# Delta-rule decoder on one core: a POOL inverse held behind the next pair's key norms, more buffers for queries and P, and join copies moved to ScalarE

## The chip, the cores and the metric

The kernel runs on one core of a Trainium2 chip. A core has a matrix engine (TensorE, in the profile PE, with its weight loads as PEld), a vector engine (VectorE, DVE), an activation engine (ScalarE, ACT), a general engine (GpSimd, POOL) and a queue engine that issues DMAs (SyncE, SP). Each engine works through its own list of instructions in the order that was fixed when the program was built; engines wait for each other by semaphores. The metric is device microseconds for one execution of the whole program, and lower is better.

## What is computed

One decoder layer on x of shape 4 x 512 x 512 in float32: a gated delta-rule attention with 16 heads of 128, then a cross attention to 256 context rows, then a causal attention, then a mixture of 8 experts. The change lies in the delta rule:

```python
def step(Sstate, inputs):
    q_t, k_t, v_t, g_t, beta_t = inputs
    retrieved = jnp.einsum('bhkv,bhk->bhv', Sstate, k_t)
    error = v_t - g_t[..., None] * retrieved
    update = k_t[..., :, None] * (beta_t[..., None] * error)[..., None, :]
    Snew = g_t[..., None, None] * Sstate + update
    o_t = jnp.einsum('bhkv,bhk->bhv', Snew, q_t)
    return (Snew, o_t)
...
o = o * jax.lax.rsqrt(jnp.mean(o * o, axis=-1, keepdims=True) + EPS) * norm_w
o = o * jax.nn.silu(x @ Wg.T)
return o @ Wo.T
```

q, k and v are projections of the normalised x, passed through a causal convolution of 4 taps and silu; q and k are scaled to length 1.

## The kernel before

The 512 steps of a sequence are done in 4 chunks of 128. Within a chunk the recurrence becomes a triangular system, and its inverse is a 128 x 128 matrix per chunk and head. Heads go in pairs: 4 sequences times 8 pairs make 32 pairs, numbered m. A pair passes through these stages:

- `stage1(m)`: the projections and convolutions of k and q. For k: projection, convolution (lines 503, 511, 514), silu, transposes (546), squares with a row sum (551), then the norms of k: `ss` on VectorE (557) and five small operations on GpSimd (558 to 562: `rk`, `ee`, `ee`, `ke`, `nr`). `ee` scales a decay matrix `em` on ScalarE (line 397, called from 572); from it and from k times k, VectorE makes `at` (579), the matrix to be inverted. It is stored to DRAM (580), and its 32 x 32 diagonal blocks are loaded as `iA` (633). Then come the q side, P (`pt`, 601), the gated q (`qg`, 590) and the norms of q (`rq`, 610 to 623).
- `stage2_inverse(m)`: 31 elimination steps on 32 partitions, each a multiplication (644) and an addition (645). Even pairs do them on VectorE, odd pairs on GpSimd. Then `iT` is stored (648), transposed by a copy (649) and stored (650), and whole squares are loaded back as `T` (653) and `X` (655).
- `stage2_values(m)`: the projections of v and of the gate (`gs`).
- `stage3(m)`: the joins put the 32 x 32 blocks together to a 128 x 128 inverse: four groups of small matmuls (704/705, 714/716, 727, 736) with copies between them (707/708, 718 to 720, 730, 738). The first group needs `T`, the second `X`. Then the row `rrow` with the norms of q is loaded (742), the gate is multiplied by it on GpSimd (745), and the four chunks follow (758 to 787), each a chain through TensorE, VectorE and ScalarE. Line 796 makes `og`.
- `output(m)`: the output projection of a pair (825), summed up in `xa`; after the last pair of a sequence, the scaling and the residual (843) and the store (845).

`prologue(b)` normalises the next sequence. Round m of the loop at line 920 writes out `stage3(m)` and, in turns with its steps, `output(m-1)`, `stage1(m+2)`, `stage2_values(m+1)` and `stage2_inverse(m+1)`: in each turn `stage1` and the inverse go two steps and the others one. The key norms of pair m+2 are written out in the sixth turn, ahead of that turn's inverse steps, which are numbers 10 and 11 of 31.

That is the order of the program. The framework's planner then fixes the list of each engine at build time: it goes by the order of the program, but puts a later instruction first where it expects an earlier one to be still waiting, by its own estimate of how long things take. So the elimination of pair m+1, which is ready early, runs about a round ahead of its place in the program. A tile name with `bufs=n` has n buffers, and a new tile waits until the last reader of the oldest is done.

Of the kernel before, what the change touches and what calls it, by code (L numbers as in the profile page):

```python
# [31 lines left out]
F32 = mybir.dt.float32  # L32
AF = mybir.ActivationFunctionType
ALU = mybir.AluOpType
# [4 lines left out]
P = 128  # L39
B, S, D = 4, 512, 512  # L40
NT = B * S // P
TB = S // P
# [56 lines left out]
def decoder(ctx: ExitStack, tc: tile.TileContext, a: dict, out: bass.AP):  # L99
# [39 lines left out]
    def chain(*gs):  # L139
        for g in gs:  # L140
            yield from g
# [27 lines left out]
    def idle(n):  # L169
        for _ in range(n):  # L170
            yield
# [154 lines left out]
    with ExitStack() as st:  # L326
# [64 lines left out]
        def chunks(t):  # L391
            return t.rearrange("p c j -> p (c j)")
# [8 lines left out]
        def prologue(b):  # L401

            x = []
            for c in range(TB):
                t = w2.tile([P, D], F32, name="x_in", bufs=4)
                nc.sync.dma_start(t, x_t[:, b * TB + c, :])
                x.append(t)
            yield
            yield
            for c, t in enumerate(x):  # L410
                run(layernorm(t.unsqueeze(1), t.unsqueeze(1), small))
                if c == 0:
                    xnT = s2.tile([P, KD, S], F32, name="xnT", bufs=2)
                    seqs[b] = [xnT]
                tp = p_b.tile([P, KD, P], F32, name="pb")
                for kd in range(KD):
                    nc.tensor.transpose(tp[:, kd, :], t[:, kd * P : (kd + 1) * P], ident)
                nc.scalar.copy(xnT[:, :, c * P : (c + 1) * P], tp)
                yield
            pab = p_b.tile([P, TB, 32], F32, name="pb")  # L420
# [101 lines left out]
        def stage1(m):  # L522
# [38 lines left out]
            nc.gpsimd.tensor_tensor(ke, ee, flat(gend), ALU.mult)  # L561
            nc.gpsimd.tensor_tensor(nr, ss, rk, ALU.mult)
            em = []
# [7 lines left out]
            for p in range(HG):  # L571
                scale(em[p], em[p], ee, p)
                pk = p_b.tile([P, TB, P], F32, name="pb")
                for c in range(TB):
                    k_ = kT[p][:, c * P : (c + 1) * P]
                    nc.tensor.matmul(pk[:, c, :], k_, k_, start=True, stop=True)
                at = live.tile([P, TB, P], F32, name="at", bufs=6)
                ats.append(at)
                nc.vector.scalar_tensor_tensor(at, pk, -1.0, em[p], ALU.mult, ALU.mult)  # L579
                nc.sync.dma_start(squares(at_d[m % SLOTS][p * TB : (p + 1) * TB]), at)  # L580
                yield
# [4 lines left out]
            for p in range(HG):  # L586
                q = s1.tile([P, S], F32, name="qh")
                yield from conv(b, hg, p, 0, wq, q)
                g = live.tile([P, S], F32, name="qg", bufs=4)
                nc.gpsimd.tensor_tensor(g, q, mb[p], ALU.mult)  # L590
                qg.append(g)
                t = w2.tile([P, S], F32, name="cv", bufs=5)
                nc.scalar.activation(t, q, AF.Square)
                sq.append(t)
                yield
                pq = p_b.tile([P, TB, P], F32, name="pb")
                for c in range(TB):
                    cs = slice(c * P, (c + 1) * P)
                    nc.tensor.matmul(pq[:, c, :], kT[p][:, cs], q[:, cs], start=True, stop=True)
                t = live.tile([P, TB, P], F32, name="pt", bufs=4)  # L600
                nc.vector.tensor_tensor(t, pq, em[p], ALU.mult)
                pt.append(t)
                yield
# [21 lines left out]

        inverses = {}

# [8 lines left out]
        def stage2_inverse(m):  # L636

            nb = HG * TB * 4
            A, T, W, ats = inverses.pop(m)
            eng = nc.vector if m % 2 == 0 else nc.gpsimd  # L640
            for i in range(31):
                n, w = 31 - i, i + 1
                u = W[:, : n * w].rearrange("p (a b) -> p a b", a=n)
                eng.tensor_tensor(u, A[:, i, i + 1 :].unsqueeze(2).to_broadcast([nb, n, w]), T[:, i, :w].unsqueeze(1).to_broadcast([nb, n, w]), ALU.mult)  # L644
                eng.tensor_tensor(T[:, i + 1 :, :w], T[:, i + 1 :, :w], u, ALU.add)  # L645
                yield
            dT, dX = inv_d[m % 2]
            nc.sync.dma_start(blocks(dT), T)
            eng.tensor_copy(A, T.rearrange("p t j -> p j t"))
# [3 lines left out]
            nc.sync.dma_start(t, squares(dT))  # L653
# [36 lines left out]
        def stage3(m):  # L690
# [15 lines left out]
            for p in range(HG):  # L706
                nc.vector.tensor_copy(Yd[p][32:64, :, 0:32], py[lo[p]])
                nc.scalar.copy(Yd[p][96:128, :, 32:64], py[hi[p]])
# [8 lines left out]
            for p in range(HG):  # L717
                nc.vector.tensor_copy(Ts[p][32:64, :, 0:32], px[lo[p], :, 64:96])
                nc.scalar.copy(Xs[p][0:32, :, 32:64], px[lo[p], :, 0:32])
                nc.vector.tensor_copy(Xs[p][64:96, :, 96:128], px[hi[p], :, 32:64])  # L720
            yield
# [21 lines left out]
            rb = [t[:, p, :] for p in range(HG)]  # L743
            for p in range(HG):
                nc.gpsimd.tensor_tensor(gs[p], gs[p], rb[p], ALU.mult)

            st_ = [None] * HG
            po = [p_o.tile([P, TB, P], F32, name=f"po{p}") for p in range(HG)]
            for c in range(TB):
# [34 lines left out]
                for p in range(HG):  # L784
                    nc.tensor.matmul(po[p][:, c, :], us[p], pt[p][:, c, :], start=True, stop=c == 0)
                    if c > 0:
                        nc.tensor.matmul(po[p][:, c, :], st_[p], qg[p][:, cs], start=False, stop=True)
                st_ = nst
                yield

# [19 lines left out]
        def output(m):  # L810
# [21 lines left out]
            if hg == NHG - 1:  # L832
# [8 lines left out]
                for c in range(TB):  # L841
                    xr = xs[c]
                    nc.vector.scalar_tensor_tensor(xr, xa[c], rs[:, c : c + 1], xr, ALU.mult, ALU.add)

                    (nc.gpsimd if m == NP - 1 else nc.sync).dma_start(x1d[b * TB + c], xr)
                    yield

        def prepare():

            ctx_ = [w2.tile([P, D], F32, name="og", bufs=2) for _ in range(2)]  # L850
            for kt in range(2):
                nc.sync.dma_start(ctx_[kt], a["ctx"][kt * P : (kt + 1) * P])
            wk = [w2.tile([P, D], F32, name="x_in", bufs=4) for _ in range(KD)]
            for kd in range(KD):
# [65 lines left out]
        for m in range(NP):  # L920
# [15 lines left out]
            if m:  # L936
                rest.append((output(m - 1), 1))
            if m + 2 < NP:
# [586 lines left out]
```

## Time and profile before

| what | value |
| --- | --- |
| time, median of 3 executions | 3873.22 us (3867.34 to 3873.66) |
| the profiled execution | 3875.28 us, its span 3873.5 us |
| busy: PE, DVE, ACT, POOL | 90%, 58%, 39%, 35% of the span |
| granted PE clock, mean over the span | 0.945 of full speed |
| part with the delta rule | from the start to about 2160 us |
| first join matmuls of pairs 2 and 30 | 272.0 us and 2078.5 us: 28 rounds in 1806.5 us |

The page gives busy times, the chain that ended last and groups of instructions. For a change to the order of work the views by time are of more use: the timeline of one engine, the list of who waited for whom in a stretch, and the busy time and granted clock by stretches. A wait of one engine costs time only where it ends in a wait of the engine that sets the pace.

### The profile page before, as it was taken

What the parts mean: (1) busy time and instruction counts of PE and PEld (TensorE: products, weight loads), DVE (VectorE), ACT (ScalarE), POOL (GpSimd) and SP (SyncE); (2) the same over time, 40 slices, a digit from 0 to 9 for tenths busy, and PEclk for the clock granted to TensorE, in tenths of its full rate; (3) what the DMA queues carried; (4) which work ended last, traced back from release to release, by engine and by line L of the source; (5) the groups of instructions that cost most, each with busy time, mean ns of one, the idle gap of its engine ahead of it and who ended that gap; (6) DMA issues with size and microseconds to landing.
All of it is one profiled execution on the core that took longest, in us unless ns stands there. A gap on an engine that the chain in (4) does not pass through costs nothing. (4 is left out here: it accounts for less than half of the span.)

```text
span 3873.5 us, 48929 instructions
## 1 busy us (share of the span) xinstructions
PE 3479.9 (90%) x16466; PEld 1984.5 (51%) x16466; DVE 2238.7 (58%) x5115; ACT 1523.7 (39%) x4190; POOL 1374.0 (35%) x1941
## 2 busy tenths in 40 slices
PE   5898989898989898989889879999999999898897
PEld 3455555555555555555545445555555555554443
DVE  5576657765766676657665546655665565554111
ACT  3334443334443434343433334444444444344121
POOL 1543554355335543554355222213212221211442
PEclk8899999998999999999999889999999999999898
DMA  5324332433234324333433245445544444456444
GB/s 163 109 71 126 104 103 78 130 104 114 78 106 129 104 77 120 105 102 100 120 88 111 72 154 161 139 147 158 163 132 140 145 139 141 137 174 206 82 82 92
DMA packets 391881, 465.56 MB, mean 120 GB/s; under 512 B 128451, under 2 KB 242115, under 8 KB 391440
## 3 DMA queue, kind: packets, MB, share of 16 engines
q1 hardware_dynamic: 380080, 438.03, 37.8%
q0 software_dynamic: 10112, 21.58, 3.1%
q8 instruction: 132, 2.16, 0.2%
q10 hardware_dynamic: 1440, 2.84, 0.2%
q14 instruction: 117, 0.96, 0.1%
HBM read 401.76 MB, written 64.81 MB: 120 GB/s over the span
## 5 line engine op out<-in xcount | busy, mean ns | idle before, releaser
L503 PE MATMUL pb<-xnT,w 128*128 128x512 f32 x2048 | 953.0, 604 | 0.0
L503 PEld LDWEIGHTS pb<-xnT,w 128*128 128x128 f32 x2048 | 381.0, 195 | 421.9 <-issue 417.8
L514 DVE SCALAR_TENSOR_TENSOR cv<-pb,pp,cv 128x511 f32<-128x511 f32 (+2 forms) x576 | 427.6, 742 | 153.0 <-ACT cv L511 144.0
L1067 PE MATMUL pb<-c_q,hT 128*128 128x512 f32 x768 | 360.7, 608 | 7.4 <-DMA c_q<-in_c_wq_dram 3.4
L644 POOL TENSOR_TENSOR iW<-iA,iT 32x31 f32<-32x31 f32 (+15 forms) x496 | 249.4, 503 | 212.3 <-DMA iA<-at_d 142.2
L825 PE MATMUL pb<-wot,og 128*128 128x512 f32 x512 | 265.9, 644 | 31.8 <-DVE og L796 26.5
L645 POOL TENSOR_TENSOR iT<-iT,iW 32x31 f32<-32x31 f32 (+15 forms) x496 | 275.2, 555 | 38.9
L511 ACT ACTIVATE cv<-pb,pp 128x512 f32<-128x512 f32 x192 | 148.2, 772 | 259.9 <-PE pb L503 259.4
L1173 PE MATMUL pw<-c_o,oT 128*128 128x512 f32 x512 | 241.8, 603 | 2.9 <-DVE oT L1165 2.9
L1067 PEld LDWEIGHTS pb<-c_q,hT 128*128 128x128 f32 x768 | 143.5, 195 | 165.4 <-issue 152.3
L1139 ACT ACTIVATE e<-pb,nm,rq 128x128 f32<-128x128 f32 (+3 forms) x256 | 157.0, 618 | 142.4 <-DVE nm L1137 108.8
L274 POOL TENSOR_SCALAR x_e<-x_e 128x1024 f32<-128x1024 f32 x64 | 68.7, 1074 | 329.4 <-ACT x_e L269 240.4
L644 DVE TENSOR_TENSOR iW<-iA,iT 32x31 f32<-32x31 f32 (+15 forms) x496 | 177.9, 359 | 12.4 <-DMA iA<-at_d 0.9
L645 DVE TENSOR_TENSOR iT<-iT,iW 32x31 f32<-32x31 f32 (+15 forms) x496 | 176.0, 355 | 11.9
L1163 PE MATMUL po<-eT,val 128*128 128x512 f32 x320 | 170.2, 625 | 6.9 <-ACT eT L1161 3.8
L558 POOL TENSOR_TENSOR rk<-ss,mhalf 128x8 f32<-128x8 f32 x32 | 53.1, 1658 | 317.9 <-DVE ss L557 317.8
L579 DVE SCALAR_TENSOR_TENSOR at<-pb,em 128x512 f32<-128x512 f32 x64 | 44.3, 692 | 208.5 <-ACT em L397 208.5
L1133 PE MATMUL pb<-kT,qT 128*128 128x256 f32 (+3 forms) x576 | 162.7, 409 | 0.8 <-ACT x_e L269 0.8
L269 ACT ACTIVATE x_e<-pb,nm 128x256 f32<-128x256 f32 x256 | 118.2, 477 | 101.9 <-DVE nm L266 101.9
L995 POOL TENSOR_TENSOR rope_s<-q,tab 128x128 f32<-128x128 f32 x64 | 35.4, 552 | 319.7 <-DVE q L1097 281.0
L825 PEld LDWEIGHTS pb<-wot,og 128*128 128x128 f32 x512 | 90.9, 197 | 110.3 <-issue 54.2
L397 ACT ACTIVATE em<-em,ee 128x128 f32<-128x128 f32 x256 | 78.6, 388 | 172.4 <-POOL ee L560 172.4
(324 smaller groups left out, 6742.1 us busy)
## 6 DMA issues: line engine op xcount, KB each, us to landing
c_o<-in_c_wo_dram SPq DMA_DIRECT2D x128, 512.0 KB, 4.1
c_q<-in_c_wq_dram SPq DMA_DIRECT2D x128, 512.0 KB, 4.7
w<-in_a_w_dram SPq DMA_DIRECT2D x124, 512.0 KB, 3.7
row<-g_d SPq DMA_DIRECT2D x64, 512.0 KB, 3.8
at_d<-at SPq DMA_DIRECT2D x64, 256.0 KB, 3.7
T<-t_d SPq DMA_DIRECT2D x32, 512.0 KB, 6.2
X<-x_d SPq DMA_DIRECT2D x32, 512.0 KB, 6.4
rrow<-r_d SPq DMA_DIRECT2D x32, 512.0 KB, 4.9
```

What stands on the lines that cost most here:

```text
L269: nc.scalar.activation(e[:, n, :], ps[r][:, g, :], AF.Exp, bias=nm[:, n : n + 1], accum_out=ssum[:, n : n + 1])
L503: nc.tensor.matmul(pj, wt[:, kd, p * P : (p + 1) * P], xnT[:, kd, :], start=kd == 0, stop=kd == KD - 1)
L511: nc.scalar.activation(ac, pj, AF.Identity, bias=cb[:, m, h : h + 1], scale=cw[:, m, h, 3:4])
L514: nc.vector.scalar_tensor_tensor(ac[:, j:], pj[:, : S - j], cw[:, m, h, 3 - j : 4 - j], ac[:, j:], ALU.mult, ALU.add)
L644: eng.tensor_tensor(u, A[:, i, i + 1 :].unsqueeze(2).to_broadcast([nb, n, w]), T[:, i, :w].unsqueeze(1).to_broadcast([nb, n, w]), ALU.mult)
L645: eng.tensor_tensor(T[:, i + 1 :, :w], T[:, i + 1 :, :w], u, ALU.add)
L825: nc.tensor.matmul(pw, og[p][:, c * P : (c + 1) * P], wot[:, p, :], start=p == 0, stop=p == HG - 1)
L1067: nc.tensor.matmul(pj, hT[:, kd, :], w[:, kd % 2, :], start=kd == 0, stop=kd == KD - 1)
L1133: nc.tensor.matmul(ps[:, m, k * P : (k + w) * P], qT[g][:, n + m, :], kT[:, g, j : j + w, :], start=True, stop=True)
L1139: nc.scalar.activation(e[n + m][:, :nk], ps[:, m, :nk], AF.Exp, bias=nm[:, n + m : n + m + 1], scale=rq, accum_out=es[:, n + m : n + m + 1])
L1163: nc.tensor.matmul(po, val[:, g, :], eT, start=k == 0, stop=k == c)
L1173: nc.tensor.matmul(pw, oT[:, h + m, :], w[:, m, :], start=g == 0 and h + m == 0, stop=g == 3 and h + m == 3)
```

## The change

Seven edits go together.

1. The last norm instruction of each pair (`nr`, 562) is remembered, and the elimination steps of odd pairs from 3 on are written out under `tc.issue_after(norms_[-1])`. That adds an edge of order alone: on GpSimd's list these steps come behind the norm instruction that was written out last. For steps 0 to 9 of pair m+1 this is the pair's own; for steps 10 to 30 it is that of pair m+2.
2. The two gate products (745) move from ahead of the chunks to the ends of chunks 1 and 2, under the same rule.
3. `qg` and `pt` get six buffers instead of four, and `at` four instead of six.
4. `x_in` has two buffers instead of four: rows 2 and 3 of a sequence are loaded when rows 0 and 1 have been used, in `prologue` and in `output`. The first prologue takes two tiles named `xa`, and the scaled sum is now written into `xa`.
5. The six join copies of a pair that VectorE made (707, 718, 720) go to ScalarE.
6. `prepare` keeps four weight tiles in `qg` and `pt` buffers instead of `x_in`.
7. `output(m-1)` starts one turn later.

```diff
-            for c in range(TB):
-                t = w2.tile([P, D], F32, name="x_in", bufs=4)
+            def load(c):
+                t = w2.tile([P, D], F32, name="xa", bufs=4) if b == 0 and c > 1 else w2.tile([P, D], F32, name="x_in", bufs=2)
                 nc.sync.dma_start(t, x_t[:, b * TB + c, :])
                 x.append(t)
+            for c in range(TB if b == 0 else 2):
+                load(c)
...
                 nc.scalar.copy(xnT[:, :, c * P : (c + 1) * P], tp)
+                if b > 0 and c + 2 < TB:
+                    load(c + 2)
...
-            nc.gpsimd.tensor_tensor(nr, ss, rk, ALU.mult)
+            norms_.append(nc.gpsimd.tensor_tensor(nr, ss, rk, ALU.mult).ins)
...
-                at = live.tile([P, TB, P], F32, name="at", bufs=6)
+                at = live.tile([P, TB, P], F32, name="at", bufs=4)
...
-                g = live.tile([P, S], F32, name="qg", bufs=4)
+                g = live.tile([P, S], F32, name="qg", bufs=6)
...
-                t = live.tile([P, TB, P], F32, name="pt", bufs=4)
+                t = live.tile([P, TB, P], F32, name="pt", bufs=6)
...
-                eng.tensor_tensor(u, A[:, i, i + 1 :].unsqueeze(2).to_broadcast([nb, n, w]), T[:, i, :w].unsqueeze(1).to_broadcast([nb, n, w]), ALU.mult)
-                eng.tensor_tensor(T[:, i + 1 :, :w], T[:, i + 1 :, :w], u, ALU.add)
+                with tc.issue_after(norms_[-1]) if m % 2 and m > 1 else ExitStack():
+                    eng.tensor_tensor(u, A[:, i, i + 1 :].unsqueeze(2).to_broadcast([nb, n, w]), T[:, i, :w].unsqueeze(1).to_broadcast([nb, n, w]), ALU.mult)
+                    eng.tensor_tensor(T[:, i + 1 :, :w], T[:, i + 1 :, :w], u, ALU.add)
...
-                nc.vector.tensor_copy(Yd[p][32:64, :, 0:32], py[lo[p]])
+                nc.scalar.copy(Yd[p][32:64, :, 0:32], py[lo[p]])
...
-                nc.vector.tensor_copy(Ts[p][32:64, :, 0:32], px[lo[p], :, 64:96])
+                nc.scalar.copy(Ts[p][32:64, :, 0:32], px[lo[p], :, 64:96])
                 nc.scalar.copy(Xs[p][0:32, :, 32:64], px[lo[p], :, 0:32])
-                nc.vector.tensor_copy(Xs[p][64:96, :, 96:128], px[hi[p], :, 32:64])
+                nc.scalar.copy(Xs[p][64:96, :, 96:128], px[hi[p], :, 32:64])
...
-            for p in range(HG):
-                nc.gpsimd.tensor_tensor(gs[p], gs[p], rb[p], ALU.mult)
...
+                if 0 < c <= HG:
+                    with tc.issue_after(norms_[-1]):
+                        nc.gpsimd.tensor_tensor(gs[c - 1], gs[c - 1], rb[c - 1], ALU.mult)
                 yield
...
+            def load(c):
+                xs.append(w2.tile([P, D], F32, name="x_in", bufs=2))
+                nc.sync.dma_start(xs[c], x_t[:, b * TB + c, :])
             if hg == NHG - 1:
-                for c in range(TB):
-                    xs.append(w2.tile([P, D], F32, name="x_in", bufs=4))
-                    nc.sync.dma_start(xs[c], x_t[:, b * TB + c, :])
+                load(0)
+                load(1)
...
-                    xr = xs[c]
-                    nc.vector.scalar_tensor_tensor(xr, xa[c], rs[:, c : c + 1], xr, ALU.mult, ALU.add)
+                    xr = xa[c]
+                    nc.vector.scalar_tensor_tensor(xr, xr, rs[:, c : c + 1], xs[c], ALU.mult, ALU.add)
+                    if c + 2 < TB:
+                        load(c + 2)
...
-            wk = [w2.tile([P, D], F32, name="x_in", bufs=4) for _ in range(KD)]
+            wk = [live.tile([P, S], F32, name="qg", bufs=6) for _ in range(2)]
+            wk += [chunks(live.tile([P, TB, P], F32, name="pt", bufs=6)) for _ in range(2)]
...
-                rest.append((output(m - 1), 1))
+                rest.append((chain(idle(1), output(m - 1)), 1))
```

More of the change, by code (lines that the diff above doesn't have):

```diff
@@ L403, in prologue @@
             x = []
-            for c in range(TB):
-                t = w2.tile([P, D], F32, name="x_in", bufs=4)
+            def load(c):
+                t = w2.tile([P, D], F32, name="xa", bufs=4) if b == 0 and c > 1 else w2.tile([P, D], F32, name="x_in", bufs=2)
                 nc.sync.dma_start(t, x_t[:, b * TB + c, :])
                 x.append(t)
+            for c in range(TB if b == 0 else 2):
+                load(c)
             yield
             yield
-            for c, t in enumerate(x):
+            for c in range(TB):
+                t = x[c]
                 run(layernorm(t.unsqueeze(1), t.unsqueeze(1), small))
@@ L624, in stage1 @@
             keys[m] = (kT, kd_, qg, pt, nr, rq)
-        inverses = {}
+        inverses, norms_ = {}, []
         def load_blocks(m, ats):
```

## The prediction

> **What bounds the kernel now.** The page comes first: TensorE is busy for nine tenths of the span, so what can be won is its waits and the clock that it is granted. The change touches the delta rule alone; I take the 28 rounds between the first join matmul of pair 2 (272.0 us) and that of pair 30 (2078.5 us), and the list of waits of that stretch (total us, times, longest).
>
> ```profile
> PE 3479.9 (90%) x16466; PEld 1984.5 (51%) x16466; DVE 2238.7 (58%) x5115; ACT 1523.7 (39%) x4190; POOL 1374.0 (35%) x1941
> ```
>
> ```profile
> PE ps L777 <- ACT u L769: 50.2, 11, 6.5
> PE ps L767 <- DVE r L760: 32.7, 36, 1.5
> PE pb L825 <- DVE og L796: 24.6, 25, 1.0
> PE pb L727 <- DVE cv L514: 21.2, 12, 2.3
> ...
> PE ps L758 <- DVE state L782: 8.4, 7, 2.3
> ```
>
> The largest wait comes eleven times, only in even rounds. The timelines of VectorE, GpSimd and SP show one case:
>
> ```profile
> 689.82 0.17 DVE L557 TENSOR_SCALAR ss<-ss 128x8 f32<-128x8 f32 x1 [1.34 <-ACT pb L551]
> ```
>
> ```profile
> 657.95 0.58 POOL L644 TENSOR_TENSOR iW<-iA,iT 32x231 f32<-32x231 f32 x1
> ...
> 678.56 0.24 POOL L622 TENSOR_SCALAR rq<-rq 128x8 f32<-128x8 f32 x1
> ...
> 689.91 0.24 POOL L645 TENSOR_TENSOR iT<-iT,iW 32x31 f32<-32x31 f32 x1
> 690.22 1.95 POOL L649 COPY iA<-iT 32x1024 f32<-32x1024 f32 x1
> 692.25 2.61 POOL L805 TENSOR_TENSOR acc<-acc,cv 128x512 f32<-128x512 f32 x2
> 695.13 2.48 POOL L745 TENSOR_TENSOR gs<-gs,rrow 128x512 f32<-128x512 f32 x2 [0.27 <-DMA rrow<-r_d]
> 697.57 1.65 POOL L558 TENSOR_TENSOR rk<-ss,mhalf 128x8 f32<-128x8 f32 x1
> ```
>
> The sums of pair 10's keys are ready at 690.0, but GpSimd first ends pair 9's inverse, its copy, two sums and two gate products; the norms start 7.6 us late. ScalarE and VectorE queue behind them, and TensorE stands 6.17 us at line 777. The clock then pays again (columns: busy us per engine, granted PE clock, DMA share, GB/s):
>
> ```profile
> 697.00:703.20 6.20, 0.04 (x1) 0.04 (x1) 1.51 (x3) 3.35 (x11) 2.94 (x6) 0.81 1.04 347
> 703.20:714.50 11.30, 10.84 (x44) 9.73 (x45) 8.47 (x18) 4.34 (x11) 1.01 (x1) 0.50 0.52 151
> 714.50:729.50 15.00, 15.00 (x62) 8.29 (x60) 13.10 (x42) 4.82 (x11) 2.90 (x4) 1.00 0.45 142
> ```
>
> After the gap TensorE works 11.3 us at half speed. Last, where the inverse is needed: it ends at 690.15, is stored, and loaded as T from 694.03 on (6.2 us to landing by the page), so T is there at 700.2, 10.1 us after the end; pair 9's join first needs it at 729.53. There are 29 us of slack.
>
> ```profile
> 694.03 0.37 SPq L653 DMA_DIRECT2D T<-t_d  x1
> ```
>
> ```profile
> 729.53 0.22 PE L704 MATMUL pb<-T,at 128*32 128x32 f32 x1
> ...
> 730.99 1.98 PE L825 MATMUL pb<-wot,og 128*128 128x512 f32 x4 [1.00 <-DVE og L796]
> ```
>
> **Edit 1, the even rounds.** The norms are no longer late. But what is pinned is 21 of 31 steps, from step 10 (the first row with 231 elements, at 657.95), and GpSimd must now stand from about 658 until the sums at 690. All that follows the sums: the five norm operations, 2.5 us (697.57 to 700.1); the steps, 27.4 us (32.2 from 657.95 to 690.15, less 4.7 for rq and qg, which slip in today; reckoned so, the other odd pairs give 26.6 to 27.6); the two gate products, which are written out between steps 15 and 22, 2.5 us; store and load, 10.0. T lands 42.4 us after the sums, where the join today starts 39.5 after them here (33.5 to 40.8 in the other rounds without a prologue), and without the late norms TensorE would be there at about 30, as in odd rounds (29.3 to 33.2). So the wait at 777 goes, and a longer one at line 704 takes its place. TensorE does not fill it with other work: its order is fixed by the planner, which takes GpSimd for much faster than it is. rq, whose copies SP had issued by 659.7, stands at 678.56 on GpSimd's list; the sums of line 805, whose squares ended at 666.5, stand behind the copy. Behind 704 the output (825) and the next key projection (503) wait as well.
>
> An even round then lasts 27.7 us from its first join to the sums (mean of 14), less 1.0 (edit 7), plus 42.4: 69.1. Fourteen of them make 967; today they make 943.2 (eleven at a mean of 65.2 and three with a prologue, 74.6, 76.8 and 74.7). With two `ln_rs` of 0.55 in each prologue round that is +27. Bounds: with the gate products outside the chain -35; T at 8.5 (2.3 for the store, 6.2 for the load) to 10.8 us, -21 to +11. I take the full sum, since the program's order puts the products inside.
>
> **SP and the queues passed.** The store (648) and loads (653, 655) move back on SP by some 32 us. Behind them wait weight loads (494), wanted a round later, and rq's copies (614), wanted 30 us later; I cost them at nothing, hidden by the standing join. The load of the next even pair's blocks (633) is a rival below. `a_rs` and `ln_rs` (123) can stand among the pinned steps, up to 9 us late; the standing join, about 12 us, covers them.
>
> **Edit 5.** Six copies a pair of 0.284 us on VectorE become six of 0.257 on ScalarE, 1.5 us a pair beside 39% busy. Line 727 no longer waits behind `cv`: 21.2, and 2.8 for `T` itself, all in odd rounds, 24.0. Without cover the longer chain on ScalarE would cost up to 0.5 us a group; 7 us of projections between the groups cover it.
>
> **Edit 7.** The waits of 825 for `og`, 1.0 each, go: eleven in odd rounds, 10.8; the even ones are counted above.
>
> **Edits 3, 2, 4, 6.** Six buffers free VectorE of its waits at `pt` (94.4 us in the stretch); with the standing join, when VectorE works ahead, I take half of the waits at 767 and 758 in odd rounds (24.2), 12.1; bounds 0 and 24. The products of odd pairs cost nothing: GpSimd idles there over 10 us. The late x loads (4.5 us to landing) lie under the standing join in three sequences; the last one, at 2199, has the loads of the next stage behind it, and I take 3 us of its 4.5. `prepare` moves loads at the start only; 0, between -5 and +5.
>
> **The clock in odd rounds.** The long wait now ends just before them. Today they lose 2.4 us each (mean clock 0.96 over 61.7). I take one stretch of 3.4 us at half speed after each join wait, 1.7, as the 1.09 us wait at 742.8 is followed by 3.4 us at 0.50, and half of today's loss: 2.9, +0.5 each, +7. Bounds: none, and 11.3 us as above, 5.65 each, +55 more.
>
> The Trainium skill ("TensorE: Matmul & The Clock Gate", Part 1) says that one idle window of about 3.4 us throttles the engine and one busy window releases it. By that rule every join wait of 12 us halves the clock and costs 1.7 us after it, the value taken; the row at 703.2 contradicts it, since TensorE was busy 10.84 of 11.30 us and stayed at half. With the row's 5.65 the sum would end at +45. I stay with the short one because 512-column matmuls (825, 503) follow the join, and at 714 the release came with them.
>
> **The sum.** +27 (even) -24.0 -10.8 -12.1 +7 +3 = -10. The profiled execution took 3875.28 us, 2.06 above the median shown; 3865 on its scale, 3863 on the median's.
>
> **The rivals.**
> 1. The clock decides (slower). It stays at half for 11.3 us after each join wait: +55 on the forecast, 3918. It passes the mark of slower when each wait costs 1.3 us more than I took. For it: 703.2 to 714.5. Against: the wide matmuls.
> 2. SP decides (slower). If load 633 of pair m+2 stands behind the store 648 on SP, VectorE's inverse starts 35 us after the sums (32.4 and 2.6) instead of 24.3 today (714.3 less 690.0). X of pair 10 lands about 5 us before its join today, so 6 us a pair, +84: 3947. Against: `at` is ready some 4 us after the norms, and 633 follows it by 7.
> 3. The join is not late, because fewer steps are pinned or other work is put ahead of 704. Then 50.2 (777), 16.1 (the wait of 423 behind ScalarE), 14 of `og` and about half of the even rounds' clock loss (5.3 each, 37) go as well, about -160: 3713. Against: the write order above.
> 4. The edge does not bind; the norms stay late. Then only edits 3, 5 and 7 count, about -50: 3823.
>
> **How the numbers follow.** Forecast 0.53 (3820 to 3920 by its bounds), rivals 0.17, 0.10, 0.12, 0.08. A measurement of this kernel can't tell less than 0.2% (7.7 us) from no change. Of the forecast's share half lies below that, 0.2 within, 0.3 above; with rivals 3 and 4 faster gets 0.47, same 0.11, slower 0.42. 3800 to 3935 leaves out rival 3, most of rival 2 and little else.
>
> **What would show it.** `rk` within 0.2 us of `ss` in even rounds; GpSimd idle some 30 us before it; the waits at 777 and 727 gone; a wait for T at 704 of about 12 us in odd joins, even rounds near 69 us and odd ones near 59. I am wrong if 704 does not wait, if the planner orders TensorE anew around it, or if `at` or `iA` of even pairs come later than today.

## The result, and the profile after

The changed kernel takes 3875.2 us (median of 12 executions, 3870.1 to 3884.9); the kernel before, executed beside it, takes 3871.4 us. The ratio is 1.0011 with a 95% interval from 1.0001 to 1.0021. That is no difference that counts, a tenth of a per cent on the slow side, where the forecast was 3863 us and a gain. The two profiled spans, 3873.5 before and 3871.6 after, differ by 1.9 us. The lines below are of the changed kernel, whose line numbers are 6 to 15 higher than those of the kernel before in this part: transposes of the prologue 423 (417 before), `ss` 565, `rk` 566, elimination 654 and 655, stores 658 and 660, loads of `T` and `X` 663 and 665, first join 714, `r` 768, `X` times `r` 775, gate products 799, scaling of the output 858.

First the busy times from the page of the kernel after, and then the list of who waited for whom between the first joins of pairs 2 and 30 (267.0 and 2079.9 us; columns: total us, times, longest).

```profile
PE 3445.1 (89%) x16466; PEld 1947.6 (50%) x16466; DVE 2243.0 (58%) x4923; ACT 1568.5 (41%) x4382; POOL 1379.5 (36%) x1941
```

```profile
PE ps L775 <- DVE r L768: 134.8, 46, 13.1
PE pb L714 <- DMA T<-t_d: 40.4, 8, 6.2
PE pb L607 <- ACT qh L525: 15.4, 3, 5.8
PE po L793 <- ACT u L777: 9.9, 28, 0.4
PE ps L766 <- DVE state L790: 8.2, 8, 1.9
PE pb L423 <- DVE xa L845: 2.1, 3, 0.8
```

The 50.2 us behind `u` (line 777 of the kernel before), the 24.6 behind `og` and the 21.2 of the join behind `cv` are gone. In their place stand 40.4 us for `T`, which the prediction had named, and 134.8 for `r` on VectorE, four times as much as before, which it had not. The timeline of VectorE and GpSimd around the sums of pair 10's keys, the same place that was shown of before (columns: start, duration, engine, line; in brackets the idle time before and what ended it), shows what the edge does:

```profile
674.62 0.17 DVE L565 TENSOR_SCALAR ss<-ss 128x8 f32<-128x8 f32 x1 [1.79 <-ACT pb L559]
...
674.88 1.65 POOL L566 TENSOR_TENSOR rk<-ss,mhalf 128x8 f32<-128x8 f32 x1 [15.86 <-DVE ss L565]
...
677.04 0.57 POOL L654 TENSOR_TENSOR iW<-iA,iT 32x231 f32<-32x231 f32 x1
...
677.85 1.27 POOL L799 TENSOR_TENSOR gs<-gs,rrow 128x512 f32<-128x512 f32 x1
...
705.50 0.24 POOL L655 TENSOR_TENSOR iT<-iT,iW 32x31 f32<-32x31 f32 x1
705.81 1.89 POOL L659 COPY iA<-iT 32x1024 f32<-32x1024 f32 x1
707.78 1.01 POOL L123 TENSOR_TENSOR a_rs<-rsq,mhalf 128x4 f32<-128x4 f32 x1
```

`rk` begins 0.1 us after the sums are there, where it had been 7.6 us late; GpSimd had stood idle for 15.9 us to make that possible (the prediction had some 30; `rq` and the sums of line 816 got in ahead); step 10 and all that follow come behind, and the inverse ends at 705.7, 31 us behind the sums, where it had ended 0.2 us behind them (690.15 and 690.0). In a plain even round (the one between the joins of pairs 6 and 7, from 523.1 to 591.6) the late inverse ends in a wait for `T`; the timelines of TensorE and of SP's queue:

```profile
576.85 0.80 PE L775 MATMUL ps<-r,X 128*128 128x128 f32 x2 [5.40 <-DVE r L768]
...
591.56 0.26 PE L714 MATMUL pb<-T,at 128*32 128x32 f32 x1 [5.05 <-DMA T<-t_d]
```

```profile
581.95 0.32 SPq L658 DMA_DIRECT2D t_d<-iT  x1
...
585.08 0.46 SPq L663 DMA_DIRECT2D T<-t_d  x1
```

The sums were there at 548.2, so `T` is loaded and the join starts 43.3 us after them, against the 42.4 of the prediction. TensorE does stand some 12 us, but 5.4 of them come ahead of the join, behind `r`.

The lines that the prediction did not foresee are in rounds 8, 16 and 24, those in which the last pair of a sequence is put out. Round 8 runs from 649.6 to 727.5; here are TensorE and VectorE:

```profile
710.89 0.80 PE L775 MATMUL ps<-r,X 128*128 128x128 f32 x2 [13.09 <-DVE r L768]
...
719.34 0.79 PE L775 MATMUL ps<-r,X 128*128 128x128 f32 x2 [6.51 <-DVE r L768]
```

```profile
708.82 1.75 DVE L858 SCALAR_TENSOR_TENSOR xa<-xa,a_rs,x_in 128x512 f32<-128x512 f32 x1 [19.51 <-POOL a_rs L123]
710.49 0.34 DVE L768 SCALAR_TENSOR_TENSOR r<-ps,ngam,vn 128x128 f32<-128x128 f32 x1
```

`a_rs`, the four roots of the output's norm, stands on GpSimd behind all 21 pinned steps (707.78 above). VectorE waits 19.5 us for it with the scaling, and `r`, which pair 8's chunk needs, is next on VectorE's list.

To compare whole rounds I take the time from the first join matmul of one pair to that of the next. Even rounds 4, 12 and 20 hold a prologue, 8, 16 and 24 an output, the other eight are called plain. Mean us of a round, and sums:

| | plain even (8) | prologue (3) | output (3) | even sum | odd (14) | odd sum | 28 rounds |
| --- | --- | --- | --- | --- | --- | --- | --- |
| before | 64.7 | 75.3 | 66.5 | 943.1 | 61.7 | 863.3 | 1806.4 |
| forecast | 69.1 | 70.2 | 69.1 | 970.7 | 58.8 | 823.4 | 1794.1 |
| after | 68.2 | 73.2 | 78.1 | 999.5 | 58.1 | 813.5 | 1812.9 |

Before pair 2's join the kernel after gains 5.0 us, behind pair 30's 3.4. With the 28 rounds, 6.5 us longer, that is the 1.9 us by which its span is shorter. So nothing stood still: 56 us were lost in even rounds and 50 won in odd ones.

### The profile page after: what moved, and what is told of

Read it like the earlier page. It is cut to its first block, busy times and chain, and to the rows that moved or that the text cites. A ratio compares the mean times of both kernels' runs of the same rounds, so it can differ in the third digit from the quotient of the medians.

```text
span 3871.6 us, 48770 instructions
## 1 busy us (share of the span) xinstructions
PE 3445.1 (89%) x16466; PEld 1947.6 (50%) x16466; DVE 2243.0 (58%) x4923; ACT 1568.5 (41%) x4382; POOL 1379.5 (36%) x1941
## 5 line engine op out<-in xcount | busy, mean ns | idle before, releaser
L511 PE MATMUL pb<-xnT,w 128*128 128x512 f32 x2048 | 972.5, 615 | 0.0
L654 POOL TENSOR_TENSOR iW<-iA,iT 32x31 f32<-32x31 f32 (+15 forms) x496 | 268.6, 541 | 41.1 <-DMA iA<-at_d 2.4
L840 PE MATMUL pb<-wot,og 128*128 128x512 f32 x512 | 251.1, 613 | 0.0
L655 DVE TENSOR_TENSOR iT<-iT,iW 32x31 f32<-32x31 f32 (+15 forms) x496 | 211.9, 427 | 10.3
L654 DVE TENSOR_TENSOR iW<-iA,iT 32x31 f32<-32x31 f32 (+15 forms) x496 | 204.2, 412 | 10.7
L775 PE MATMUL ps<-r,X 128*128 128x128 f32 x384 | 81.4, 311 | 139.0 <-DVE r L768 138.4
L598 POOL TENSOR_TENSOR qg<-qh,row 128x512 f32<-128x512 f32 x64 | 84.5, 1325 | 223.3 <-ACT qh L525 221.1
L775 PEld LDWEIGHTS ps<-r,X 128*128 128x128 f32 x384 | 63.1, 204 | 171.1 <-DVE r L768 149.6
```

The lines of the kernel that those rows point to most:

```text
L511: nc.tensor.matmul(pj, wt[:, kd, p * P : (p + 1) * P], xnT[:, kd, :], start=kd == 0, stop=kd == KD - 1)
L775: nc.tensor.matmul(pu, Xs[p][:, c, :], rs[p], start=True, stop=True)
L840: nc.tensor.matmul(pw, og[p][:, c * P : (c + 1) * P], wot[:, p, :], start=p == 0, stop=p == HG - 1)
```

## The experiments

The theory after the result, A: the edge works as forecast, even rounds are set by the chain from the key sums to `T`, the other edits win in odd rounds, and the miss lies in the three output rounds. Rivals were that the even rounds lose for another reason (B or C in the expectations), or that the odd rounds' gain also hangs on the edge. Each ratio is to the kernel before, executed on the same chip, with its 95% interval. The texts set off below say what was expected of each run before it was built, in the order named ahead of them.

| run | time, us | ratio | interval |
| --- | --- | --- | --- |
| after | 3875.2 | 1.0011 | 1.0001 to 1.0021 |
| e_nopin: no step pinned | 3830.3 | 0.9902 | 0.9872 to 0.9932 |
| e_pin17: steps 17 to 30 pinned | 3782.0 | 0.9774 | 0.9757 to 0.9792 |
| e_pin24: steps 24 to 30 pinned | 3738.3 | 0.9664 | 0.9645 to 0.9684 |
| e_pin_only: before, with edit 1 alone | 3922.4 | 1.0130 | 1.0113 to 1.0147 |
| e_ars: `a_rs` off GpSimd | 3861.4 | 0.9990 | 0.9980 to 0.9999 |
| e_store: stores on GpSimd's queue | 3854.1 | 0.9957 | 0.9943 to 0.9972 |
| e_ars_store: both | 3829.9 | 0.9903 | 0.9887 to 0.9920 |
| e_gates: gate products ahead | 3809.8 | 0.9856 | 0.9839 to 0.9872 |
| e_copies: edit 5 undone | 3890.3 | 1.0060 | 1.0043 to 1.0077 |
| e_noidle: edit 7 undone | 3899.4 | 1.0076 | 1.0059 to 1.0093 |
| e_buf4: buffers of edit 3 undone | 3855.6 | 0.9967 | 0.9953 to 0.9981 |
| e_pin24_store: e_pin24 and e_ars_store | 3751.2 | 0.9697 | 0.9681 to 0.9713 |
| e_best: that and the gate products ahead | 3763.1 | 0.9726 | 0.9710 to 0.9742 |

**How many steps are pinned.** Three runs change the condition alone, and one puts edit 1's pin on the steps, without anything else, into the kernel before.

```diff
-                with tc.issue_after(norms_[-1]) if m % 2 and m > 1 else ExitStack():
+                with tc.issue_after(norms_[-1]) if False else ExitStack():                                # e_nopin
+                with tc.issue_after(norms_[-1]) if m % 2 and m > 1 and i >= 17 else ExitStack():          # e_pin17
+                with tc.issue_after(norms_[-1]) if m % 2 and m > 1 and i >= 24 else ExitStack():          # e_pin24
```

Expected of e_nopin, e_pin17, e_pin24 and e_pin_only:

> The kernel after, but the elimination steps of odd pairs are not pinned; all other edits stay. Theory A (the pin only trades the late norms for a late T at the join, and the other edits are worth some 50 us in odd rounds): norms of even rounds 5 to 8 us late again, even rounds near 65 us, no wait for T, odd rounds near 58 us, 3825 us. Rival B (the short odd rounds come from VectorE working ahead while TensorE stands at the join): odd rounds back near 62 us, 3865 us.

> The kernel after, but only steps 17 to 30 are pinned, some 17 us of elimination. Theory A: T about 33 us after the sums, at most 3 us of wait for it, even rounds near 62 us, 3790 us, between the one with step 24 and the kernel after. Rival C: even rounds near 66 us, 3840 us, no different from the one with step 24.

> The kernel after, but only steps 24 to 30 are pinned behind the next pair's norms, so some 6.5 us of elimination follow them instead of 27.4. Theory A: norms on time, T about 22 us after the sums, no wait at the join, even rounds near 61 us, 3770 us. Rival C (with T in time the wait for r on VectorE, 5.4 us in even rounds of the kernel after, takes its place in full): even rounds near 66 us, 3840 us.

> The kernel before with the pin on the elimination steps of odd pairs alone (from 3 on), without the other edits; the gate products are not pinned. Theory A: norms on time, T late at the join, even rounds near 67 us and near 76 in rounds 8, 16 and 24, odd rounds near 62 us: 3910 us. Rival D (the pin is neutral by itself and the other edits are worth nothing): 3872 us, odd rounds 58 us already here.

e_nopin leaves the gate products where the change puts them. Without the pin on the steps odd rounds stay at 58.7 us, so their gain does not hang on the edge; plain even rounds go back to 64.4. The waits of e_nopin (three of TensorE, one of VectorE) and of e_pin24 over the 28 rounds:

```profile
PE pb L423 <- DVE xa L845: 53.6, 3, 19.3
PE ps L785 <- ACT u L777: 49.2, 11, 5.0
PE ps L775 <- DVE r L768: 37.1, 33, 1.7
...
DVE ln_st L131 <- DMA x_in<-in_x_dram: 54.0, 3, 19.4
```

```profile
PE ps L775 <- DVE r L768: 33.4, 26, 1.9
PE pb L554 <- ACT kT L525: 18.5, 13, 1.5
PE ps L766 <- DVE state L790: 17.6, 16, 3.0
PE pb L423 <- DVE xa L845: 13.6, 3, 4.8
```

In e_nopin the late norms are back (785 behind `u`, 49.2 us, as 777 in the kernel before), and in the three prologues a wait of up to 19.3 us appears; the prologue rounds take 83.2 us. The profile puts that wait down to `xa`, which had ended long before; VectorE waits there for the rows of x (the last line of the first list). SP issues their loads at 420.97 in round 4, behind the store of the inverse (414.31) and the loads of `T` and `X`. So it is the late loads of edit 4 that TensorE stands for here, 53.6 us in all (no run undoes edit 4 by itself); in the changed kernel VectorE waits 2.5 us for these rows, in e_pin24 14.5. In e_pin24 the norms' wait is gone and the prologues' wait is down to 13.6 us, no join waits for `T` (it is there 12.2 us early in round 6), output rounds last 56.2 us and plain even rounds 57.0, 11.2 less than after. Seven pinned steps are enough to let the norms through. This is the fastest of all the versions, 3.4% faster than the kernel before, and faster than its theory A had it (3770). Against e_nopin, which has every edit but the pin, the pin on 7 steps gains 92 us and the pin on 21 steps loses 45. With 14 steps the join no longer waits either, but plain even rounds take 62.9 and output rounds 69.0. The pin alone, in the kernel before, costs 50 us: 30 in even rounds (943.1 to 973.4), and 20 in odd ones (863.3 to 883.4). Theory A had 3910 for it.

**What makes the output rounds long.** The first run takes the root on ScalarE and inverts on VectorE, the second sends an odd pair's two stores out from GpSimd's queue, the third does both.

```diff
-                rsqrt(rs, pq, small, add=1e-6, mul=1.0 / VD)
+                nc.vector.tensor_scalar(rs, pq, 1.0 / VD, 1e-6, ALU.mult, ALU.add)                       # e_ars
+                nc.scalar.activation(rs, rs, AF.Sqrt)
+                nc.vector.reciprocal(rs, rs)
...
-            nc.sync.dma_start(blocks(dT), T)
+            (nc.gpsimd if m % 2 else nc.sync).dma_start(blocks(dT), T)                                    # e_store
...
-            nc.sync.dma_start(blocks(dX), A)
+            (nc.gpsimd if m % 2 else nc.sync).dma_start(blocks(dX), A)
```

Expected of e_ars, e_ars_store and e_store:

> After, but the root of the output's norm (`a_rs`, line 859 in `output`) is taken on ScalarE and inverted on VectorE, so that it no longer stands behind the pinned steps on GpSimd. Theory A (the three rounds 8, 16, 24 are 10 us longer than the other even rounds because `a_rs` stands behind the pinned steps and VectorE's list holds `r` behind the scaling at line 858): the three rounds fall from 78.1 to about 69, the 13 us wait of TensorE for `r` there goes, 3848 us. Theory B (VectorE is late there because its elimination steps run slower beside a busy GpSimd): the three rounds stay at 77 to 78, 3875.

> The kernel of the last run with `a_rs` off GpSimd, and in addition the two stores of an odd pair's inverse (lines 658 and 660) go out from GpSimd's queue, so that SP's list no longer stands at them. Theory A (rounds 8, 16 and 24 have two late inputs behind the pinned steps, `a_rs` on GpSimd and the third x load on SP behind the store; with one of them gone the other holds VectorE for 11 us at the scaling): with both gone the three rounds fall from 74.2 to 69 or less, 3845 us. Theory B (the x load is late for its own reason, two buffers): they stay at 74, 3861.

> After, with only the two stores of an odd pair's inverse (lines 658 and 660) on GpSimd's queue in place of SP's. Theory A (in rounds 8, 16 and 24 the first wait of TensorE for `r`, 13.1 us, is `a_rs` and the second, 6.5 us, the x load behind the store on SP): the second goes and the first stays, 78.1 to about 72, 3857 us. Theory B (SP's list costs nothing, as the prediction had it): 78, 3875 or up to 15 more, since GpSimd now issues the stores ahead of its copy and each plain even round waits for T.

The first run missed: the three rounds fell from 78.1 to 74.2, not to 69. Its timelines of VectorE, TensorE and SP in round 8 say why:

```profile
691.17 2.15 DVE L860 SCALAR_TENSOR_TENSOR xa<-xa,a_rs,x_in 128x512 f32<-128x512 f32 x2
...
712.30 0.75 DVE L860 SCALAR_TENSOR_TENSOR xa<-xa,a_rs,x_in 128x512 f32<-128x512 f32 x1 [11.32 <-DMA x_in<-in_x_dram]
```

```profile
713.37 0.80 PE L775 MATMUL ps<-r,X 128*128 128x128 f32 x2 [16.58 <-DVE r L768]
```

```profile
706.50 0.32 SPq L658 DMA_DIRECT2D t_d<-iT  x1
...
708.87 0.52 SPq L832 DMA_DIRECT2D x_in<-in_x_dram  x1
```

The first two scalings (860 here) now run at 691, but the third needs a row of x. With two `x_in` buffers its load is issued only after a scaling, and by then it stands on SP behind the store of the inverse, which waits for GpSimd until 706.5. So there were two late inputs in a row, and the second took over as soon as the first was mended. e_store shows the reverse: with the store off SP and `a_rs` still behind the steps, VectorE stands 15.66 us for `a_rs`, TensorE waits once and for 19.1 us, and the rounds take 78.9 where I had written 72.

```profile
703.42 2.48 DVE L858 SCALAR_TENSOR_TENSOR xa<-xa,a_rs,x_in 128x512 f32<-128x512 f32 x1 [15.66 <-POOL a_rs L123]
```

```profile
712.90 0.80 PE L775 MATMUL ps<-r,X 128*128 128x128 f32 x2 [19.11 <-DVE r L768]
```

With both mended the three rounds take 68.3 us, just under the forecast's 69.1 (plain rounds of this run take 65.3), and what stands last in them is what the forecast had in all even rounds, the wait for `T` (timeline of TensorE in e_ars_store, round 8):

```profile
695.59 0.49 PE L775 MATMUL ps<-r,X 128*128 128x128 f32 x2 [3.81 <-DVE r L768]
...
711.66 0.26 PE L714 MATMUL pb<-T,at 128*32 128x32 f32 x1 [7.39 <-DMA T<-t_d]
```

The stores on GpSimd's queue also shorten plain even rounds, from 68.2 to 65.3, so some 3 of the 6 us from 74.2 to 68.3 need not be the x row's. In round 6 of e_ars_store the load of `T` lands 3.8 us behind its issue, in the changed kernel 6.4 us, where the load of `X` follows it by 1.3 us instead of 6.4. That the two loads slow each other is what this suggests; it was not tested by itself, and the distance alone does not decide: in the changed kernel `T` took 6.3 us in round 7 and 4.6 in round 4, with `X` 2.0 us behind it in both.

**The terms of the sum.** Four runs undo one part each.

```diff
-                if 0 < c <= HG:
-                    with tc.issue_after(norms_[-1]):
-                        nc.gpsimd.tensor_tensor(gs[c - 1], gs[c - 1], rb[c - 1], ALU.mult)
...
+            for p in range(HG):                                                                           # e_gates, ahead of the chunks
+                nc.gpsimd.tensor_tensor(gs[p], gs[p], rb[p], ALU.mult)
...
-                nc.scalar.copy(Yd[p][32:64, :, 0:32], py[lo[p]])
+                nc.vector.tensor_copy(Yd[p][32:64, :, 0:32], py[lo[p]])                                   # e_copies, and the two of px likewise
...
-                rest.append((chain(idle(1), output(m - 1)), 1))
+                rest.append((output(m - 1), 1))                                                           # e_noidle
...
-                g = live.tile([P, S], F32, name="qg", bufs=6)
+                g = live.tile([P, S], F32, name="qg", bufs=4)                                             # e_buf4, and pt likewise
```

Expected of e_gates, e_copies, e_buf4 and e_noidle:

> After, but the two gate products are issued ahead of the chunks and not behind the norms, as before the change. Theory A (T ends even rounds, and the products are 2.5 us of the chain from the key sums to T): T 2.5 us earlier, plain even rounds from 68.2 to about 65.7, 3847 us (the prediction's bound was 35 less). Theory B (the wait for `r` on VectorE, 5.4 us in a plain even round, sets the even round and only moves): plain even rounds stay within 0.7 of 68.2, 3872.

> After, but the joins' three copies are back on VectorE (edit 5 undone). Theory A (the prediction's term of 24.0 holds): odd rounds go from 58.1 to 59.8, 3899 us. Theory B (VectorE no longer stands behind `cv` or `pt` at the joins, or the copies are hidden): odd rounds stay within 0.4 of 58.1, 3875 (3869 to 3881). Even rounds wait for T either way, so they move by under 1.

> After, but with four buffers for `qg` and four for `pt`, as before the change. Theory A (the prediction's term of 12.1 for the buffers, in odd rounds): odd rounds from 58.1 to 59.0, 3887 us. Theory B (four buffers also hold VectorE and GpSimd back in even rounds): even rounds longer by 1 or more, over 3895. Theory C (the buffers hide nothing): 3875.

> After, without the one idle step ahead of `output` (edit 7 undone). Theory A (the prediction's term: TensorE waits 1.0 us for `og` in each round): odd rounds from 58.1 to about 59, 3886 us, and the waits of line 840 for `og` come back. Theory B (the odd rounds' further gain of 22 us, beyond the copies' 28, comes from elsewhere): odd rounds within 0.3 of 58.1, 3875.

The gate products are worth more than theory A had: plain even rounds fall from 68.2 to 62.4. The steps from number 10 to the end take 27.9 us in place of 31.4 in round 6, and the join starts 4.2 us behind the issue of the load of `T`, not 6.5; why that load lands sooner was not tested. The waits for `T` shrink to almost nothing, while those for `r` mostly stay; over the 28 rounds of e_gates (777 there is 775 of the changed kernel):

```profile
PE ps L777 <- DVE r L770: 110.7, 44, 9.4
...
PE pb L714 <- DMA T<-t_d: 3.0, 6, 1.0
```

The copies on VectorE again make the odd rounds 60.1 us, 28.4 more in all, where the term was 24.0 (the even rounds give 8.6 back, so the whole is 15 us slower). But the wait of the join behind `cv` does not come back: of the 28.4, 10.9 are other waits (behind `state` 11.0 where the changed kernel has 4.0, behind `kT` 4.2 and `xa` 1.4, and 2.1 less behind `r`), and the rest is clock, 0.939 of full speed in odd rounds against 0.959. Without the idle step the odd rounds take 60.2 us, 29.3 more, so edit 7 does help; but the mechanism that I named, a wait for `og`, does not come back. The waits of e_noidle:

```profile
PE pb L714 <- DMA T<-t_d: 27.9, 10, 3.8
PE ps L766 <- DVE state L790: 21.4, 25, 1.3
...
PE pb L840 <- DVE og L807: 0.2, 1, 0.2
```

Sorted by rounds, all of the `T` waits end even rounds; 12.6 us of the `state` waits and 6.7 behind `kT` lie in odd rounds, which the changed kernel has as 4.0 and 0; the rest is clock (0.944 against 0.959 of full speed in odd rounds). Four buffers, last, are faster than six beside the pin: 3855.6 us. No theory had that, and its cause stays open. Odd rounds stay at 57.9, and plain even rounds fall to 66.3; in round 6 GpSimd needs 29.4 us from step 10 to the end, not 31.4.

**Two versions on top of the shorter pin.** The last two runs put the repairs on top of e_pin24, with (e_best) and without (e_pin24_store) the gate products ahead of the chunks, by the diffs shown. In the second text below "the kernel of the last call" is e_best.

> After, with the pin on steps 24 to 30 alone (3738 us by itself), the gate products ahead of the chunks, `a_rs` off GpSimd and an odd pair's stores on GpSimd's queue. Theory A (with seven pinned steps T is 10 us early, a_rs and the x loads are 2 us late at most, so nothing of this is on the path): 3730 to 3742 us. Theory B (each piece gives back what it gave in the kernel with 21 pinned steps, 63 for the products and up to 30 for the rest): below 3700.

> The pin on steps 24 to 30 alone, with `a_rs` off GpSimd and an odd pair's two stores on GpSimd's queue, the gate products left where the change puts them. Theory A (the gate products ahead of the norms cost the kernel of the last call its 25 us, since `rk` came 2.3 us late; the other two pieces are neutral or better here): 3725 to 3745 us. Theory B (the other two pieces cost them): about 3763.

Neither helps: 3763 and 3751 against 3738. With the products ahead, they stand in front of the norms again, and `rk` is 1.1 to 3.0 us late in most even rounds (GpSimd in e_best, sums ready at 545.3):

```profile
545.13 2.50 POOL L755 TENSOR_TENSOR gs<-gs,rrow 128x512 f32<-128x512 f32 x2 [2.00 <-DMA rrow<-r_d]
547.60 1.64 POOL L566 TENSOR_TENSOR rk<-ss,mhalf 128x8 f32<-128x8 f32 x1
```

That accounts for part: without it plain even rounds are back near e_pin24 (57.7 against 57.0), yet output rounds stay at 62.4 against 56.2. In those three VectorE waits 8.2 us for the rows of x again and TensorE 14.6 for `r`, where e_pin24 has 0 and 2.1; why the rows come late there was not followed further. A mend for a wait is no gain where the wait is gone.

**VectorE beside GpSimd.** The elimination on VectorE was slower in the changed kernel than before, so one run put a probe ahead of the work.

```diff
+        probe(nc.vector, 0)
+        nc.vector.memset(zW, 0.0)
+        probe(nc.gpsimd, 1)
+        probe(nc.vector, 0)
...
+        probe(nc.gpsimd, 1)
+        probe_psum()
```

Expected of e_port:

> After, with a probe ahead of the work, on tiles of zeros: 12 pairs of elimination steps of 32x231 on VectorE alone; the same with 12 pairs on GpSimd beside them; 12 operations of 128x512 with one input in PSUM on VectorE alone; the same with GpSimd's steps beside them; GpSimd's steps alone. Theory A (VectorE's operations with both inputs in SBUF are slowed by a GpSimd at work, those with an input in PSUM are not): the 32x231 steps take 0.36 to 0.40 us alone and 0.6 to 0.7 beside GpSimd, the PSUM form 0.74 in both. Theory B (the longer steps of the changed kernel come from elsewhere): 0.36 to 0.40 in both. The time of the whole is that of after and some 70 us for the probe.

The planner mixed the probe with the first work of the kernel, so the 24 PSUM operations all ran without GpSimd beside them, and the 32x231 steps beside GpSimd were interrupted: 0.37 to 0.39 us alone, 0.37 to 0.83 beside it. The clear rows are, by chance, those of the kernel's own softplus, which fell beside GpSimd's steps there and stands alone in the changed kernel. The timelines of VectorE and GpSimd in the probe's run, and then that of VectorE in the changed kernel, where GpSimd did nothing at that time:

```profile
62.87 0.73 DVE L555 SCALAR_TENSOR_TENSOR cv<-pb,pp,cv 128x509 f32<-128x509 f32 x1
63.53 2.80 DVE L480 SCALAR_TENSOR_TENSOR sp_y<-sp_y,sp_w 128x64 f32<-128x64 f32 x5
66.36 0.67 DVE L483 SCALAR_TENSOR_TENSOR sp_y<-sp_y,sp_z 128x64 f32<-128x64 f32 x1
67.06 0.59 DVE L484 TENSOR_SCALAR sp_y<-sp_y 128x64 f32<-128x64 f32 x1
...
66.32 0.63 POOL L392 TENSOR_TENSOR iT<-iT,iW 32x231 f32<-32x231 f32 x1
67.03 0.57 POOL L391 TENSOR_TENSOR iW<-iA,iT 32x231 f32<-32x231 f32 x1
```

```profile
30.89 0.74 DVE L522 SCALAR_TENSOR_TENSOR cv<-pb,pp,cv 128x509 f32<-128x509 f32 x1
...
31.77 1.78 DVE L447 SCALAR_TENSOR_TENSOR sp_y<-sp_y,sp_w 128x64 f32<-128x64 f32 x7
33.59 0.23 DVE L450 SCALAR_TENSOR_TENSOR sp_y<-sp_y,sp_z 128x64 f32<-128x64 f32 x1
33.85 0.20 DVE L451 TENSOR_SCALAR sp_y<-sp_y 128x64 f32<-128x64 f32 x1
```

The same instructions take three times as long (0.67 for 0.23, 0.59 for 0.20) beside GpSimd, each ending just after one of its steps; the operation that reads PSUM takes 0.73 and 0.74.

## Why the prediction was right and wrong

- **The late norms and the edge: right.** `rk` begins 0.1 us after `ss` in all even rounds, the wait at 777 is gone, and the wait for `T` at the join is there.
- **The even round: right for a plain one.** From its first join to the sums 25.2 us (26.7 forecast: 27.7 less 1.0), from the sums to the next join 43.0 (42.4): 68.2 against 69.1. My figure for the wait at 704, about 12 us, is right only as a sum: 4.3 to 6.2 at the join, and before it some 1.4 and 4.2 to 5.4 behind `r`, since VectorE was late too.
- **"`a_rs` and `ln_rs` (123) can stand among the pinned steps, up to 9 us late; the standing join, about 12 us, covers them": this is the step that failed.** `a_rs` was not among the steps but behind all of them. Its input was there at 687.6 and its result at 708.8, 21 us later. And the cover was not there: the scaling holds VectorE's list, `r` of the running chunk stands behind it, and the chunk comes before the join, so the loss adds to the round and does not hide under its last wait. The three output rounds took 78.1 us instead of 69.1, 27 us in all, which turns a forecast of -10 into +17.
- **"The late x loads lie under the standing join" and SP "at nothing": failed with it.** I gave each queue that the store was moved past its own cost and looked at one load behind it, 633; the load that mattered was the x row of edit 4, behind the store in the output rounds. e_ars shows it alone (74.2), e_ars_store the rounds without either (68.3), and in e_nopin VectorE waits 54.0 us for such rows in the three prologues. Rival 2 had the right queue and the wrong load; the elimination of even pairs was not held up as it had it (plain rounds were as forecast).
- **The prologue rounds** took 73.2 where the sum has 70.2, 9 us in all. In rounds 4, 12 and 20 `T` is early by 6.6 us or more and a wait of 4.8 to 5.8 for `qh` (607) stands there; what delays `qh` was not tested.
- **The odd rounds: near in size, -50 for -40, by partly wrong terms.** TensorE's waits there, before and after: the join behind `cv` and `T` 24.0 to 0, and `og` 10.8 to 0, as the terms of edits 5 and 7 said. But undoing edit 5 costs 28.4 and undoing edit 7 29.3, both by other waits and the clock: neither wait comes back when its edit alone is undone. So each edit helps, and that the sizes are near the terms is no proof of their mechanism; which edits together removed those two waits stays open. The term for the buffers was wrong: `r` and `state` together were 24.2 and are 24.9, so the 12.1 that I took for half of them did not come, and e_buf4 shows that the buffers cost time beside this edge. In their place came 11.5 that I had not counted (`kT` 6.8, `xa` 4.7).
- **The clock: half right.** In the row after a join's wait the clock was at half for 3.5 us and at 0.91 over the next 7.8, some 4.9 us at half speed, not 11.3; over the 20 us behind each of the eight joins that waited it was 3.3 to 5.9, so rival 1 fell. But odd rounds lost nothing against before (0.959 and 0.960), so the +7 did not come either. The rows (columns: busy us per engine, granted PE clock, DMA share, GB/s):

```profile
591.50:595.00 3.50, 3.44 (x36) 1.83 (x37) 1.89 (x5) 2.17 (x6) 0.00 (x0) 0.50 1.07 333
595.00:602.80 7.80, 7.80 (x47) 3.76 (x46) 3.97 (x7) 2.63 (x8) 4.41 (x4) 0.91 0.44 158
```

- **Start and end:** -5.0 and -3.4, where I had 0 and +3.

Together: even +56 for +27, odd -50 for -40, start and end -8 for +3; -2 for -10. The forecast landed 12 us from the median by luck, because a miss of 29 us on one side met misses of 10 and 11 on the other; the reasons held for the plain even rounds and failed in the three output rounds, which cost 27 of the 29. Rival 3 ("fewer steps are pinned", 3713) is what e_pin24 makes come true, at 3738.

## What to carry to other kernels

An edge of order that holds back a long run of instructions holds back everything that was written out behind them on that engine, and on the DMA queue that waits for their result: list those readers round by round, the rare rounds too, and ask of each whether its reader sits on another engine's list ahead of the critical work. A wait at the end of a round covers only what is needed at the end. Pin as little as lets the urgent instruction through: with all other edits the same, 7 pinned steps gained 92 us and 21 lost 45. And an edit that is undone alone shows what it is worth, not why: look whether the wait that it was to remove comes back.

## What the runs showed of the hardware

Operations of VectorE with both inputs in SBUF ran longer while GpSimd ran its elimination steps or operations of 128x512: one of 128x64 took 0.67 us instead of 0.23. In the changed kernel the multiplications of the elimination of 32x192 took 0.62 us on average beside a busy GpSimd and 0.34 without it, those of 32x231 0.68 and 0.39 (means of those with over 80% and with under 5% of their time beside a GpSimd instruction). GpSimd's steps of 32x231 stretched in turn, from 0.57 to up to 0.84 us in the probe's run. Operations of 128x511 with an input in PSUM took 0.74 in both cases.

One kind of GpSimd instruction slowed nothing. Beside its `pow` operations on 128x8 (566 and 631, 1.7 us), which read SBUF too, the 89 elimination steps of VectorE that fell there in e_pin24 took what they take alone, as here:

```profile
571.74 1.72 POOL L631 TENSOR_TENSOR rq<-rq,mhalf 128x8 f32<-128x8 f32 x1
...
571.97 0.39 DVE L654 TENSOR_TENSOR iW<-iA,iT 32x231 f32<-32x231 f32 x1
```

The Trainium skill ("SBUF — State Buffer", "Who interferes with whom") says that an instruction of VectorE with two inputs in SBUF contends with one of GpSimd that reads SBUF, under an exclusive lock, and that one with at most one such input does not, outside the modes that use both ports. The two-input rows beside the elimination agree with it, and so does the 0.74; the rows beside `pow` show no lock for the length of the instruction. The row of TENSOR_SCALAR, one input in SBUF and 0.59 instead of 0.20, would be the page's other case, the mode with two ports, which no run here tells apart.

The edge put the two eliminations side by side: of VectorE's 868 steps in the 28 rounds, counting those with over 80% of their time beside a step of GpSimd's elimination, there were none before, 178 after, and none in e_pin24. The waits for `r` outside the output rounds were 31.6, 74.2 and 31.3 us. In round 6 the 18 steps that VectorE runs from 562.4 to the late `r` at 576.5 take 9.7 us, and the same shapes alone 5.0 (means of the trace): by this estimate 4.7 of the 5.4 us that TensorE waits there. No run changes this alone. It does not explain why four buffers beat six: in e_buf4 203 steps ran side by side, and the waits for `r` came to 134.2 us.
